# Six strips in work over eight slots, TensorE kept in program order, and masked queries on ScalarE in a line-attention stage

## The chip, the cores and the metric

The kernel runs on one core of a Trainium2 chip. The metric is the device time of one execution in microseconds; three executions of the kernel before had a median of 8827.78 us (8826.51 to 8828.34). All data are float32.

The core has a matrix engine (TensorE, PE), a vector engine (VectorE, DVE), an activation engine (ScalarE, ACT), a general engine (GpSimd, POOL) and a queue that issues loads (SyncE, SP). Each works through its own list of instructions in order; semaphores hold an instruction until what it needs is there. TensorE writes to PSUM[...]; the other engines read from there and copy to SBUF.

## The reference

Two layers act on an image `x` of shape (4, 64, 256, 256). The first is a convolution block: layer norm, attention over channels, a gated local branch, then a feed-forward part that ends with a transform of 8 x 8 patches: forward DFT, a weight per frequency, inverse DFT. The second layer is a pair of linear attentions along image lines, first along rows, then along columns, and a two-layer MLP. What matters here is the end of the first layer and the row attention:

```python
        y = gelu(x_gate) * concatenate([x1_2, x2], 1)
        y = _conv1x1(y, out_w)
        ...
        f = jnp.fft.rfft2(p) * fW
        p = jnp.fft.irfft2(f, s=(P, P))
...
    q = elu(x @ wq.T + bq) + 1        # 4 heads, 1 value per head
    k = elu(x @ wk.T + bk) + 1
    v = x @ wv.T + bv                 # 4 heads, 16 values per head
    q = q / q.mean(over the line);  k = k / k.sum(over the line)
    ktv = einsum('brhcd,brhce->brhde', k, v)
    o = einsum('brhcd,brhde->brhce', q, ktv)
    h = xe + o @ wo.T + bo            # xe: the layer's input, x: xe normalized
```

## The kernel before

The program is one fully unrolled list, in five stages that follow one another: `stage_a` and what ends it (attention of the first layer, up to about 1720 us), `stage_c1` (to about 3400 us), `stage_c2` (to about 5040 us), `stage_c3`, the middle stage that is changed (5050 to 6672 us), and `stage_d` (column attention and MLP, to the end). `stage_c3` does the 1x1 convolution `out_w`, the patch transform with the residual, and the row attention. It reads `yd` and `xmd` from DRAM and writes `hd`.

Its unit of work is a strip: 8 image rows of a pair of images. There are 2 pairs and 32 strips in each, so 64 strips, `seq`. A strip passes five generators, one turn of the loop after another:

- `product`: the convolution, 4 row pairs with two matmuls each (L970, one for each image, each 64 columns of the array wide), a ScalarE copy each (zc, L971); then 16 transposes in four groups (L980) with a copy each (zs, L981).
- `patches`: for both halves of the strip, the forward DFT (L997, two PSUM tiles), times the frequency weights on VectorE (fs, L1001, two), the inverse DFT (L1007, two tiles), the addition of the residual (xe, L1010, two), and the statistics of a layer norm on VectorE and ScalarE (s L1013, xc L1015, square L1017, sv L1018); at the end the root on ScalarE and the reciprocal (rs, L1021 and L1023).
- `features`: four rounds of four transposes (L1033), a copy (xrT, L1035) and four matmuls of scores (L1038), all into one tile qk; then on VectorE the transpose qp (L1043), scale (u, L1045), bias (L1047), the feature map (fe L695, exponential on ScalarE L696, f L1050), kr (L1056), and the masked forms: kx by eight ScalarE instructions (L1058), qx by one GpSimd instruction (L1059); the sums fr (L1061) and, on VectorE, kj and qj twice (L1065, L1066).
- `attend`: 32 small matmuls of keys with values (L1079), the two sums over the line (L1081, L1082), rz and qr (L1084, L1086), zn (L1089), eight transposes of qx (L1095) with copies qT (L1096), a fold (L1100), zT (L1102), and, in the helper `mix`, a matmul (L702), m4 (called m in the profile, L708), its sum mx_m (L710), and then bdm (L1106).
- `update`: four tiles that are first filled with the bias by four matmuls (L1115), then eight matmuls (L1119); VectorE adds xe (h, L1121) and GpSimd issues four transfers to `hd` (L1125).

Turn n runs `patches` of strip n-1, `update` of n-4, `attend` of n-3, `features` of n-2 and `product` of n, in this order, and `_steps` takes one step of each in rotation, from `yield` to `yield`, until all are done. Loads for strip n+1 are issued by SP at the turn's start (ya L955, xmp L957). A scheduler then places the instructions of all engines: it may move an instruction ahead of others of its engine, and did so with TensorE's: in the program as built the four row-pair products of L970 stand as one matmul, then four of L1038, then three of L970.

PSUM has two pools: six tiles tagged `mm` that all matmul groups take in rotation, in the order in which the code asks for them, and two tagged `sm` for qk and zp. SBUF pool `pf` has two buffers for most names, three for xe, one for zc and h1.

Of the kernel before, what the change touches and what calls it, by code (L numbers as in the profile page):

```python
# [249 lines left out]
def kernel(ctx: ExitStack, tc: tile.TileContext, x, packs, fd, out, off):  # L250
# [670 lines left out]
    def stage_c3():  # L921
        NS = H // 8
        with ExitStack() as cs:
# [33 lines left out]
                SY.dma_start(xmp, xmd[pr, s])  # L957
                ld[pr, s] = ya, xmp

            zss, xes, fes, bds = {}, {}, {}, {}  # L960

            def product(pr, s):

                ya, _ = ld[pr, s]

                zc = p.tile([128, 32, 32, 2], F32, name="zc", bufs=1)
                for r in range(4):
                    t = mm()
                    for b in (0, 1):
                        T.matmul(t[b * 64:(b + 1) * 64, :], owT, ya[:, :, 2 * r:2 * r + 2, b * 64:(b + 1) * 64].rearrange("p f y t -> p y f t"), start=True, stop=True)  # L970
                    S.copy(zc[:, :, 8 * r:8 * r + 8].rearrange("p j f t -> p f j t"), t.rearrange("p (f j t) -> p f j t", f=8, t=2))  # L971
                    if r % 2:
                        yield
                zs = p.tile([128, 16, 2 * C], F32, name="zs")
                zss[pr, s] = zs
                for k in range(4):
                    t = mm()
                    for i in range(4):
                        j = 2 * (4 * k + i)
                        T.transpose(t[:, i * 128:(i + 1) * 128], zc[:, j:j + 2].rearrange("p j f t -> p (j f t)"), ident)  # L980
                    S.copy(zs[:, 4 * k:4 * k + 4].rearrange("p g c -> p (g c)"), t)  # L981
                    if k % 2:
                        yield

            def patches(pr, s):

                _, xmp = ld.pop((pr, s))
                zs = zss.pop((pr, s))
                xe = p.tile([128, 16, 2 * C], F32, name="xe", bufs=3)
                sv = p.tile([128, 32], F32, name="sv")  # L990
                for hf in (0, 1):

                    zh = zs[:, 8 * hf:8 * hf + 8].rearrange("p (n g) c -> p n (g c)", n=2)
                    ts = [mm(), mm()]
                    for pt in (0, 1):
                        for n in (0, 1):
                            T.matmul(ts[pt][n * 64:(n + 1) * 64, :], dfw[pt * 64:(pt + 1) * 64, :], zh[pt * 64:(pt + 1) * 64, n], start=True, stop=True)  # L997
                    fs = []
                    for pt in (0, 1):
                        f_ = p.tile([128, 512], F32, tag=f"fs{pt}", name=f"fs{pt}", bufs=1)  # L1000
                        V.tensor_tensor(f_.rearrange("p (g c) -> p g c", c=C), ts[pt].rearrange("p (g c) -> p g c", c=C), mid_bc(fw, 8), ALU.mult)  # L1001
                        fs.append(f_)
                    yield
                    ts = [mm(), mm()]
                    for pt in (0, 1):
                        for n in (0, 1):
                            T.matmul(ts[n][pt * 64:(pt + 1) * 64, :], dfi[n * 64:(n + 1) * 64, :], fs[pt][n * 64:(n + 1) * 64, :], start=True, stop=True)  # L1007
                    for n in (0, 1):
                        r = slice(8 * hf + 4 * n, 8 * hf + 4 * n + 4)
                        V.tensor_tensor(xe[:, r].rearrange("p g c -> p (g c)"), ts[n], xmp[:, r].rearrange("p g c -> p (g c)"), ALU.add)  # L1010
                    src = xe[:, 8 * hf:8 * hf + 8].rearrange("p g (b c) -> p (g b) c", b=2)
                    s1 = p.tile([128, 16], F32, name="s1")
                    V.tensor_reduce(s1, src, AX.X, ALU.add)  # L1013
                    xc = p.tile([128, 16, C], F32, name="xc")
                    V.scalar_tensor_tensor(xc, bc(s1, C), -LN_S, src, ALU.mult, ALU.add)  # L1015
                    sq = p.tile([128, 16, C], F32, name="sq")
                    S.activation(sq, xc, AF.Square)  # L1017
                    V.tensor_reduce(sv[:, 16 * hf:16 * hf + 16], sq, AX.X, ALU.add)  # L1018
                    yield
                sd = p.tile([128, 32], F32, name="sd")  # L1020
                S.activation(sd, sv, AF.Sqrt, bias=eps_t, scale=LN_S)  # L1021
                rs = p.tile([128, 32], F32, name="rs")
                V.reciprocal(rs, sd)  # L1023
                xes[pr, s] = xe, rs

            def features(pr, s):

                xe, rs = xes[pr, s]
                qk = sm()
                for k in range(4):  # L1030
                    t = mm()
                    for i in range(4):
                        T.transpose(t[:, i * 128:(i + 1) * 128], xe[:, 4 * k + i], ident)  # L1033
                    xT = p.tile([128, 512], F32, name="xrT")
                    S.copy(xT, t)  # L1035

                    for g in range(4):
                        T.matmul(qk[g * 32:(g + 1) * 32, k * 128:(k + 1) * 128], rw, xT.rearrange("p (j n) -> p j n", j=4)[:, :, g * 32:(g + 1) * 32],  # L1038
                                 start=True, stop=True)
                    yield  # L1040

                qp = p.tile([128, 16, 32], F32, name="qp")
                V.transpose(qp.rearrange("p j m -> p (j m)"), qk)  # L1043
# [12 lines left out]
                V.tensor_tensor(kr, f[:, :, 4:8], bc(rs, 4), ALU.mult)  # L1056
                for y in range(8):
                    S.activation(kx[:, :, y], kr, AF.Identity, scale=rmask[:, y:y + 1])  # L1058
                G.tensor_tensor(qx, f[:, :, 0:4].unsqueeze(2).to_broadcast([128, 32, 8, 4]), mk.to_broadcast([128, 32, 8, 4]), ALU.mult)  # L1059
                fr = p.tile([128, 2, 8], F32, name="fr")  # L1060
                V.tensor_reduce(fr, f.rearrange("p (j b) h -> p b h j", b=2), AX.X, ALU.add)  # L1061
                qj = p.tile([128, 2, 2, 8, 4], F32, name="qj")
# [6 lines left out]
            def attend(pr, s):  # L1069

                xe, _ = xes.pop((pr, s))
                qx, kx, qj, kj = fes.pop((pr, s))
                yield
                zp = sm()

                for j in range(16):
                    for b in (0, 1):
                        g = (2 * b + j % 2) * 32
                        T.matmul(zp[g:g + 32, :64], kx[:, 2 * j + b].rearrange("p y h -> p (y h)"), xe[:, j, b * 64:(b + 1) * 64], start=(j < 2), stop=(j >= 14))  # L1079
                qs = mm()  # L1080
                T.matmul(qs[:, 0:1], qj.rearrange("p d b y h -> p (d b y h)"), K0("ones"), start=True, stop=True)  # L1081
                T.matmul(qs[:, 1:2], kj.rearrange("p b d y h -> p (b d y h)"), K0("ones"), start=True, stop=True)  # L1082
                rz = p.tile([128, 1], F32, name="rz")
                V.reciprocal(rz, qs[:, 1:2])  # L1084
                qr = p.tile([128, 1], F32, name="qr_")
                V.tensor_copy(qr, qs[:, 0:1])  # L1086
                zn = p.tile([128, 65], F32, name="zn")
                G.memset(zn[:, 64:65], 0.5)
                V.tensor_scalar(zn[:, 0:64], zp[:, 0:64], rz, None, ALU.mult)  # L1089
                qT = p.tile([128, 1024], F32, name="qTr", bufs=1)  # L1090
                for k in (0, 1):
                    t = mm()
                    for i in range(4):
                        j = 8 * k + 2 * i
                        T.transpose(t[:, i * 128:(i + 1) * 128], qx[:, 2 * j:2 * j + 4].rearrange("p a y h -> p (a y h)"), ident)  # L1095
                    S.copy(qT[:, k * 512:(k + 1) * 512], t)  # L1096
                yield
                t = mm()

                T.matmul(t[:65, :64], zn, K("rfold"), start=True, stop=True)  # L1100
                zT = p.tile([65, 2, 64], F32, name="zT")
                V.tensor_copy(zT, mid_bc(t[:65, :64], 2))  # L1102
                yield
                m = mix(p, zT.rearrange("p j y -> p (j y)"), rgt, qr)
                bdm = p.tile([128, 4, 64], F32, name="bdm")
                V.tensor_tensor(bdm, mid_bc(m, 4), bc(K("jmask"), 64), ALU.mult)  # L1106
                bds[pr, s] = xe, qT, bdm

            def update(pr, s):

                xe, qT, bdm = bds.pop((pr, s))
                h1 = p.tile([128, 2, 16, C], F32, name="h1", bufs=1)
                ts = [mm() for k in range(4)]
# [9 lines left out]
                for b in (0, 1):  # L1123
                    for a in (0, 1):
                        G.dma_start(hd[2 * pr + b, 8 * s:8 * s + 8, 8 * a:8 * a + 8], h1[a * 64:(a + 1) * 64, b])  # L1125
                yield

            seq = [(pr, s) for pr in range(B // 2) for s in range(NS)]
            load(*seq[0])

            for n in range(len(seq) + 4):
                if n + 1 < len(seq):
                    load(*seq[n + 1])
                _steps(*(f(*seq[n - d]) for d, f in ((1, patches), (4, update), (3, attend), (2, features), (0, product)) if 0 <= n - d < len(seq)))

    stage_c3()

# [272 lines left out]
```

## Time and profile before

| What | Value |
|---|---|
| median of three executions | 8827.78 us |
| profiled execution, its own time | 8823.91 us |
| its span | 8822.1 us |
| mean granted TensorE clock | 0.971 |
| TensorE busy | 8201.0 us, 93% |
| VectorE busy | 5913.9 us, 67% |
| ScalarE busy | 4597.9 us, 52% |
| GpSimd busy | 1205.3 us, 14% |
| first L970 to last L1121 (the middle stage) | 5051.6 to 6671.6 us |
| L1079 in it, 4096 matmul records | 219 ns each |
| L1059 in it, 64 instructions on POOL | 1967 ns each |

The span is the time from the first to the last instruction of the profiled execution; what lies around it (1.8 us here) belongs to the execution's own time. A float32 matmul makes two matmul records in the profile, a transpose one. Records overlap:[...] the step from one start to the next is the better measure of what it costs TensorE. PE is the matmul engine and PEld its weight loads. A row of the timeline has start, length, engine, line, operation, output and inputs, and in brackets the idle time before it and what ended it. A row of the waits has who waited, for whom, the total in us, how often and the longest.

### The profile page before, as it was taken

Reading aid. Unit: us, or ns where it says so; the run is one execution under the profiler, and the core shown is the slowest. Engines: PE = TensorE matmul, PEld = TensorE weight load, DVE = VectorE, ACT = ScalarE, POOL = GpSimd, SP = SyncE. Lnnn points to the kernel's source line nnn. Section 1 sums busy time; section 2 is a strip of 40 time slices with the busy share of each in tenths; the row PEclk is TensorE's granted clock in tenths of the full one; section 3 lists DMA queues with packets and bytes.
Section 4 is the critical chain, followed back from the end, with each engine's and each line's share of the span. In section 5 each row is a group of like instructions: output and inputs, shape, how many; then the busy total and the mean of one; then the engine's idle time right before and its main releaser. Section 6 shows DMA issues by size and latency. Waiting matters only on the chain. (4 is left out here: it accounts for less than half of the span.)

```text
span 8822.1 us, 143300 instructions
## 1 busy us (share of the span) xinstructions
PE 8201.0 (93%) x57518; PEld 4222.1 (48%) x57518; DVE 5913.9 (67%) x8506; ACT 4597.9 (52%) x7781; POOL 1205.3 (14%) x1828
## 2 busy tenths in 40 slices
PE   8999999699999998999999999999997999999998
PEld 6777777344444443333333344444444444444443
DVE  7766666377777774222222288888887788887886
ACT  4455455455555553222222266666664777777776
POOL 1111111212222221000000011111110101001011
PEclk9999999699999999999999999999997999999999
DMA  7777777799999998888888855555542323333232
GB/s 163 160 188 189 178 185 179 195 351 391 397 386 392 388 388 315 299 295 299 295 299 295 279 174 167 169 168 172 170 142 71 68 58 76 59 66 69 58 76 40
DMA packets 1258502, 1832.48 MB, mean 208 GB/s; under 512 B 335600, under 2 KB 1040112, under 8 KB 1196656
## 3 DMA queue, kind: packets, MB, share of 16 engines
q1 hardware_dynamic: 1053296, 1034.63, 39.0%
q0 software_dynamic: 204544, 788.69, 28.0%
q8 instruction: 456, 7.47, 0.3%
q14 instruction: 206, 1.69, 0.1%
HBM read 967.65 MB, written 788.53 MB: 199 GB/s over the span
## 5 line engine op out<-in xcount | busy, mean ns | idle before, releaser
L915 DVE TENSOR_TENSOR y<-ge,mm 128x512 f32<-128x512 f32 (+1 forms) x640 | 406.0, 635 | 1211.9 <-ACT ge L914 1211.8
L882 PE MATMUL mm<-t,w 128*128 128x512 f32 (+1 forms) x2560 | 1093.9, 566 | 19.4 <-DMA t<-td 19.4
L914 ACT ACTIVATE ge<-mm 128x512 f32<-128x512 f32 (+1 forms) x640 | 354.9, 555 | 1253.5 <-PE mm L889 1253.5
L775 PE MATMUL mm<-gp,wc 128*64 128x510 f32 (+1 forms) x3072 | 702.5, 595 | 91.0 <-DVE xm L785 51.7
L620 PEld LDWEIGHTS mm<-wqk,gp 128*128 128x128 f32 x6144 | 728.8, 197 | 99.4 <-issue 61.5
L882 PEld LDWEIGHTS mm<-t,w 128*128 128x128 f32 x2560 | 455.4, 190 | 647.9 <-issue 437.2
L620 PE MATMUL mm<-wqk,gp 128*128 128x128 f32 x6144 | 762.5, 282 | 1.1 <-POOL gp L589 0.9
L1341 ACT ACTIVATE hg<-mm,b 128x512 f32<-128x512 f32 x1024 | 645.2, 689 | 47.3 <-PE mm L1339 45.6
L1339 PE MATMUL mm<-xfT,w 64*128 64x512 f32 x2048 | 623.7, 626 | 25.7 <-DVE h L1309 22.6
L830 ACT COPY tb<-mm 128x512 f32<-128x512 f32 x512 | 300.7, 588 | 628.0 <-PE mm L824 620.3
L889 PE MATMUL mm<-t,w 64*64 64x504 f32 (+1 forms) x5120 | 575.6, 555 | 0.0
L824 PE MATMUL mm<-xl,pack_c 64*128 64x512 f32 x2048 | 510.6, 599 | 6.4 <-ACT xl L812 4.7
L775 PEld LDWEIGHTS mm<-gp,wc 128*64 128x64 f32 x3072 | 277.2, 137 | 471.1 <-issue 333.6
L1356 PE MATMUL mm<-hg,pack_d 128*64 128x512 f32 x2048 | 496.8, 606 | 0.0
L316 ACT ACTIVATE ln_sq<-xn 128x1024 f32<-128x1024 f32 x256 | 274.6, 1073 | 365.3 <-DVE xn L314 365.2
L1363 POOL DMA_DIRECT2D out_dram<-st x128 | 209.1, 1638 | 1725.0 <-DVE st L1357 1640.9
L318 DVE TENSOR_REDUCE ln_v<-ln_sq 128x16 f32<-128x1024 f32 x256 | 312.0, 1219 | 185.2 <-ACT ln_sq L316 185.2
L970 PE MATMUL mm<-ya,pack_e 128*64 128x512 f32 x1024 | 381.2, 616 | 11.0 <-DMA ya<-yd 11.0
L828 DVE COPY tb<-mm 128x512 f32<-128x512 f32 x512 | 344.2, 683 | 22.4 <-PE mm L824 16.9
L1339 PEld LDWEIGHTS mm<-xfT,w 64*128 64x128 f32 x2048 | 225.6, 185 | 255.2 <-issue 112.1
L1357 DVE TENSOR_SCALAR st<-mm,pack_d 128x512 f32<-128x512 f32 x256 | 277.7, 1085 | 101.3 <-PE mm L1356 101.3
L889 PEld LDWEIGHTS mm<-t,w 64*64 64x64 f32 x5120 | 158.1, 132 | 374.4 <-issue 374.4
(458 smaller groups left out, 15368.5 us busy)
## 6 DMA issues: line engine op xcount, KB each, us to landing
t<-td SPq DMA_DIRECT2D x256, 1152.0 KB, 10.1
td<-tb POOLq DMA_DIRECT2D x144, 1024.0 KB, 15.6
td<-tb POOLq DMA_DIRECT2D x288, 512.0 KB, 13.9
yd<-y POOLq DMA_DIRECT2D x128, 1152.0 KB, 10.1
ya<-yd SPq DMA_DIRECT2D x192, 512.0 KB, 5.7
xs<-in_x_dram SPq DMA_DIRECT2D x128, 512.0 KB, 6.8
projd<-pj POOLq DMA_DIRECT2D x256, 256.0 KB, 5.9
gp<-projd SPq DMA_DIRECT2D x128, 512.0 KB, 9.1
```

Of the source, the lines that this page charges most:

```text
L620: T.matmul(qp[:, k * 128:(k + 1) * 128], gp[:, 2 * i + k // 2, at + dx:at + dx + 128], wqk[:, dx, :], start=(dx == 0), stop=(dx == 2))
L775: T.matmul(tv[i * 64:(i + 1) * 64, :, o], wc[2 * pr + i][:, dx, :], gps[i][:, 2 * r:2 * r + 2, i_], start=(dx == 1), stop=False, skip_grou ...
L824: T.matmul(t, inT[q, hf * 128:(hf + 1) * 128], xls[b // 2, s][q, :, 2 * y:2 * y + 2].rearrange("p f y t -> p f (y t)"), start=True, stop=True)
L828: V.tensor_copy(o, i_)
L882: T.matmul(t[:, :n], w[:, 0:128], x_[:, c, :], start=True, stop=False, skip_group_check=True)
L889: T.matmul(t[po:po + 64, :n].rearrange("p (n c) -> p n c", c=64)[:, :, o], w[q:q + 64, 128:192], x_[q:q + 64, c, i_], start=False, stop=Tr ...
L914: S.activation(ge[:, :n], ts[0][k][:, :n], AF.Gelu)
L915: V.tensor_tensor(y[:, c, :].rearrange("p n c -> p (n c)"), ge[:, :n], ts[1][k][:, :n], ALU.mult)
L970: T.matmul(t[b * 64:(b + 1) * 64, :], owT, ya[:, :, 2 * r:2 * r + 2, b * 64:(b + 1) * 64].rearrange("p f y t -> p y f t"), start=True, sto ...
L1339: T.matmul(t, w1[rh * 64:(rh + 1) * 64, k * 128:(k + 1) * 128], xT[rh * 64:(rh + 1) * 64], start=True, stop=True)
L1341: S.activation(g, t, AF.Gelu, bias=b1[:, k:k + 1])
L1356: T.matmul(y[rh * 64:(rh + 1) * 64, :], w2[:, k, :], hg[k * 2 + rh], start=False, stop=(k == 1), skip_group_check=True)
```

## The change

The change rewrites the yields of `stage_c3`, so that a turn has eight slots, and splits `attend`: its end (the call of `mix` and bdm) becomes a sixth generator, `mixed`, which runs at the start of the next turn. `update` starts in the second slot, `features` makes its next transposes in the slot of the scores before, `attend` starts in the fifth slot. All of the loop stands in a block that takes TensorE's instructions out of the scheduler's hands: they stay as the program has them. The order of the generators in a turn changes. xe gets a fourth buffer. qx is made by eight ScalarE instructions, as kx is, in place of one on GpSimd. The matmuls and their sizes are the same.

```diff
-            zss, xes, fes, bds = {}, {}, {}, {}
+            zss, xes, fes, zts, bds = {}, {}, {}, {}, {}
...
                     S.copy(zc[...], ...)
-                    if r % 2:
+                    yield
+                    if r == 0:
                         yield
+                yield
...
-                xe = p.tile([128, 16, 2 * C], F32, name="xe", bufs=3)
+                xe = p.tile([128, 16, 2 * C], F32, name="xe", bufs=4)
...
                         fs.append(f_)
+                    yield
                     yield
...
                     V.tensor_reduce(sv[:, 16 * hf:16 * hf + 16], sq, AX.X, ALU.add)
                     yield
+                    if hf == 0:
+                        yield
...
-                for k in range(4):
+
+                def up(k):
                     t = mm()
                     for i in range(4):
                         T.transpose(t[:, i * 128:(i + 1) * 128], xe[:, 4 * k + i], ident)
                     xT = p.tile([128, 512], F32, name="xrT")
                     S.copy(xT, t)
+                    return xT
+
+                def score(k, xT):
                     for g in range(4):
                         T.matmul(qk[...], rw, xT..., start=True, stop=True)
-                    yield
+
+                xT = up(0)
+                for k in range(3):
+                    yield
+                    yield
+                    score(k, xT)
+                    xT = up(k + 1)
+                yield
+                score(3, xT)
...
-                G.tensor_tensor(qx, f[:, :, 0:4].unsqueeze(2).to_broadcast([128, 32, 8, 4]), mk.to_broadcast([128, 32, 8, 4]), ALU.mult)
+                for y in range(8):
+                    S.activation(qx[:, :, y], f[:, :, 0:4], AF.Identity, scale=rmask[:, y:y + 1])
...
-                yield
+                for k in range(4):
+                    yield
                 zp = sm()
...
+                yield
                 qs = mm()
...
                     S.copy(qT[:, k * 512:(k + 1) * 512], t)
                 yield
+                yield
                 t = mm()
...
                 V.tensor_copy(zT, mid_bc(t[:65, :64], 2))
-                yield
+                zts[pr, s] = xe, qT, zT, qr
+
+            def mixed(pr, s):
+                xe, qT, zT, qr = zts.pop((pr, s))
                 m = mix(p, zT.rearrange("p j y -> p (j y)"), rgt, qr)
...
                 bds[pr, s] = xe, qT, bdm
+                yield
...
+                yield
                 xe, qT, bdm = bds.pop((pr, s))
...
-                yield
...
-            for n in range(len(seq) + 4):
-                if n + 1 < len(seq):
-                    load(*seq[n + 1])
-                _steps(*(f(*seq[n - d]) for d, f in ((1, patches), (4, update), (3, attend), (2, features), (0, product)) if 0 <= n - d < len(seq)))
+            with tc.manual_schedule(engines={mybir.EngineType.PE}):
+                for n in range(len(seq) + 4):
+                    if n + 1 < len(seq):
+                        load(*seq[n + 1])
+                    _steps(*(f(*seq[n - d]) for d, f in ((4, mixed), (1, patches), (4, update), (2, features), (3, attend), (0, product)) if 0 <= n - d < len(seq)))
```

## The prediction, made before the changed kernel ran

> **What bounds the kernel now.** I read the page's totals and slices, then the middle stage by windows, then one turn of it in order of time, then the waits. The stage runs from the first L970 at 5051.6 us to the last L1121, at 6671.6: 1620 us for 64 turns. In full turns L702 follows L702 after 24.84 us. One turn by windows (length, then busy time of PE, weight loads, DVE, ACT, POOL, then granted clock, DMA share, GB/s):
>
> ```profile
> 5816.00:5840.84 24.84, 23.49 (x218) 12.29 (x217) 21.25 (x41) 15.45 (x29) 4.28 (x6) 1.00 0.55 170
> ```
>
> TensorE is occupied in 23.49 of 24.84 us at full clock; VectorE is next; DMA is half used. The timeline of that turn (start, length, engine):
>
> ```profile
> 5816.95 1.07 PE L970 MATMUL mm<-ya,pack_e 128*64 128x512 f32 x2
> ...
> 5818.39 0.43 PE L1038 MATMUL sm<-xrT,rw 128*32 128x128 f32 x8 [0.36 <-ACT xrT L1035]
> ...
> 5818.74 1.93 PE L970 MATMUL mm<-ya,pack_e 128*64 128x512 f32 x6
> ...
> 5820.07 1.97 POOL L1059 TENSOR_TENSOR qx<-f,pack_e 128x1024 f32<-128x1024 f32 x1
> 5820.39 1.74 DVE L1065 TENSOR_TENSOR kj<-fr,pack_e 128x64 f32<-128x64 f32 x1
> ...
> 5822.05 0.21 DVE L1066 TENSOR_TENSOR qj<-fr,pack_e 128x64 f32<-128x64 f32 x1
> ...
> 5822.39 1.10 PE L1079 MATMUL sm<-xe,kx 128*32 128x64 f32 x64 [0.69 <-ACT kx L1058]
> ```
>
> L1038 splits the two pairs of L970 products, and kj takes 1.74 us while POOL makes qx, 0.21 afterwards. The waits of 5200 to 6560 (55 turns) name what TensorE stands for:
>
> ```profile
> PEld sm L1038 <- ACT xrT L1035: 146.2, 219, 1.2
> ...
> PE sm L1079 <- ACT kx L1058: 38.2, 55, 0.7
> ...
> PE sm L1038 <- ACT xrT L1035: 19.4, 54, 0.4
> ```
>
> A last view, from the first stage, shows what a pause of TensorE does: 1.9 us without a matmul (425.8 to 427.7), then 3.4 us at half clock.
>
> ```profile
> 425.80:428.00 2.20, 0.30 (x9) 0.28 (x10) 2.17 (x4) 0.00 (x0) 0.00 (x0) 0.99 0.23 69
> 428.00:431.40 3.40, 3.40 (x35) 1.62 (x32) 1.46 (x3) 0.76 (x3) 0.00 (x0) 0.50 0.00 0
> 431.40:434.80 3.40, 3.40 (x35) 3.28 (x36) 1.62 (x2) 1.71 (x6) 0.00 (x0) 1.00 0.41 108
> ```
>
> [...]
>
> **The change, part by part.** Durations are steps from start to start in the timelines of before; lines are those of before, and the order is that of the changed program as built.
>
> *TensorE's order.* L970's four products now stand as one, two together, one, whole. Split halves cost 1.00+1.86 us twice a turn, 5.7 in all; unsplit, two products take 1.87 us (in the stage's fill, 5061.22 to 5063.09), one 1.02 (as L997): 3.9. That removes 1.8. The waits on kx (0.7), on xrT (0.4 once, 0.15 twice) and on bdm (0.15) should go too: 1.4 to 1.5. The new order's floor: L702 0.6, L997 two groups 2.0, L1007 two 2.0, L1033 four 2.3, L1038 four 1.4, L970 3.9, L1115 1.0, L1119 3.6, L1079 1.0, L1081 and L1082 0.5, L1095 1.0, L980 1.9, L1100 0.2: 21.4, with changes of shape about 21.6 us.
>
> *qx.* POOL loses 1.97 us, VectorE the 1.53 by which kj is held: 19.7 us left. (Bounds: POOL keeps its hd issues and a 0.1 us memset, so part of the 1.53 could stay, and then lies in the ring below; the second kj, beside those issues, takes 0.21, so I take all of it as gone.) ScalarE gains 8 instructions of L1058's form and size; their step is 0.29, or at most L1058's whole 0.39 if reading f, whose rows are spaced, is slower. I take 0.29: 2.3, so 17.8. They stand behind kx and ahead of the copies xrT(0) and zc(0). kr ends about 3.8 us after L702 starts; 16 x 0.29 makes 8.5, xrT 9.1, zc 9.6. The first L1007 wants xrT's buffer at 10.6 below: hidden with 1.5 us spare (0.7 at 0.39); in a 21.6 us turn it would be late. The last three hd transfers on POOL no longer stand behind qx (2.0 us earlier), and nothing waits for them. SP's loads keep their order.
>
> *xe's fourth buffer* adds no instruction; zero. Without it the first xe write would wait for the last h addition, which VectorE's order puts before it anyway.
>
> *mix in the next turn.* L702 now opens the turn, behind zT, which ends the previous turn on VectorE. Behind L702 on TensorE queue L997, L1033, L970, L1115.
>
> *The new wait.* PSUM has six mm buffers. From L702 on, they are taken by L997 (two), L1033, L970, then four by L1115; so the fourth L1115 takes the buffer that fs1 reads. VectorE's order puts that fs1 last: zT, u+bias, fe, sv, m4, fs0, f, mx_m, kr, fr, bdm, rs, kj, qj, kj, qj, fs1. L1119 stands behind that L1115, so it now waits not for bdm but for fs1; behind it waits the whole rest of the turn, and VectorE for it. This closes a ring:
>
> - VectorE, from the second half's xe to zT: xe 0.60+0.71, s 1.14, qp 0.63, xc 1.13, u 0.33, zT 0.28 = 4.8. (L1100's product is there 2 us earlier.)
> - VectorE, zT's end to fs1's: u+bias starts 0.08 before it, 0.44, fe 0.28 (it waits shortly for ScalarE's square), sv 1.12, m4 0.33, fs0 0.60, f 0.33, mx_m 0.51, kr 0.21, fr 0.50, bdm 0.33, rs 0.26, three of kj and qj 0.39, the last 0.13, fs1 0.68 = 6.0.
> - TensorE, from there to the second L1007's output: L1115 0.95, L1119 3.6, L1007 1.03, L1038 0.38, L1033 0.58, L970 1.88, L997 1.03, L1038 0.38, L1033 0.58, L1079 1.03, L970 1.01, L1081 and L1082 0.49, L1095 0.95, L1007 1.15 = 15.0.
>
> With two handovers of 0.05: 25.9 us. Inside it TensorE stands from 4.1 (three L1115 streamed) to 6.05 us after L702, 1.95 us, and from its last L980 to the next L702, 1.6 us. Ring against before: +1.1 a turn.
>
> *The clock.* The trace of before has no such pause in a full turn, so I bound this: none halved, 0; every first pause halved, 3.4 us at half rate, +1.7 a turn. [...]the second pause now and then slows the opening matmuls, which removes the first. I take 0.8 a turn, so 26.75.
>
> *Sum.* Fill and drain lose waits: the last three intervals, traced 26.3, 22.0 and 12.5, have no closed ring; I estimate -15 in all from the shorter order there (-20 to -5). 60 full turns x (26.75-24.84) = +115; +100 in sum. The other stages' orders are unchanged, so the profiled execution's 8823.91 (span 8822.1 and 1.8 around it) becomes about 8924. The median of the runs, 8827.78, lies 3.9 above that: 8928.
>
> **The rivals.**
> - *The order works* (faster). TensorE runs at its floor, with 0.3 for leftovers 21.9: 60 x (-2.94) - 15 = -191, 8637. For it: VectorE has only 19.7 us of work. Against: VectorE's order is fixed. It decides where fs1 is ready when TensorE has streamed three L1115, 4.1 us after L702 instead of 6.0, and zT 1.6 us earlier too: 3.6 us off the ring's VectorE legs.
> - *Ring without halving* (slower): 60 x 1.1 - 15 = +51, 8879. For: the pauses are just near the size that was punished.
> - *Ring, halved nearly every turn* (slower): 60 x 2.8 - 15 = +153, 8981; for: the pause repeats each turn.
> - *The ring but shorter by 0.9* (small overlaps I count too long): 60 x 0.2 - 15, about no change.
>
> **Numbers.** Ring with part of the turns halved 60%, without halving 15%, halved nearly always 12%, order works 10%, about no change 3%. The range takes in the two slower neighbours, 8868 to 8990, and leaves out 13%. What this kernel's measurement can tell from no change is 0.2%, 18 us. Slower 0.87, same 0.03, faster 0.10.
>
> **What would show it.** Right: L702 every 26 to 27.5 us; the first L1119 of a turn starting about 1 us after fs1's end and never earlier; TensorE pausing twice a turn; granted clock of the stage near 0.97 (half for 3.4 us in about half of the turns); kj at 0.21; VectorE busy about 19.7 a turn. Wrong: L702 at 22 us and L1119 right behind bdm; or VectorE taking fs1 ahead of kj. If L702 is at 25.9 throughout and the clock 1.00, only the clock's share fails.

## The result and the profile after

The changed kernel takes 9033.22 us (median of 4 runs, 9028.23 to 9041.06) against 8828.06 us (4 runs) before: a ratio of 1.0234, 95% interval 1.0219 to 1.0248. It is slower by 205 us. The forecast was slower, by 100 us, with a range that ended at 8990.

The profiled execution took 9030.88 us with a span of 9029.1. These are its totals and its clock, where before had 8201.0 us for PE and nines in the slices that now show eights:

```profile
PE 8350.0 (92%) x57518; PEld 4307.3 (48%) x57518; DVE 5864.9 (65%) x8506; ACT 4743.7 (53%) x8293; POOL 1078.5 (12%) x1764
...
PEclk9999999799999999999999988888887999999999
```

The same number of matmul records keeps TensorE busy 149 us longer, and seven slices of the middle stage stand at 8 in the clock. VectorE has 49 us less. The six of the title are generators: `mixed` and `update` take the same strip, n-4, so five strips are in work in a turn, as before. The middle stage lasts from the first L970 at 5050.8 us to the end of the last h at 6880.2, so 1829 us where it was 1620: the 209 us are all in it. Line numbers below are those of the changed kernel: L1142 is the bias matmul (L1115 before), L1146 the product with bdm (L1119), L1010 the inverse DFT (L1007), L1003 fs (L1001), L1123 zT (L1102), L1013 xe (L1010). By windows, full turns and then four successive stretches of one turn that starts at 5246.6:

```profile
5200.00:6700.00 1500.00, 1374.55 (x11394) 721.89 (x11394) 1075.09 (x2046) 929.16 (x1882) 121.80 (x264) 0.88 0.47 148
```

```profile
5246.60:5249.70 3.10, 3.10 (x18) 1.09 (x18) 3.06 (x7) 3.05 (x4) 0.00 (x0) 1.00 0.97 386
5249.70:5253.10 3.40, 1.84 (x10) 0.60 (x8) 2.76 (x10) 3.39 (x12) 0.00 (x0) 1.00 0.00 0
5253.13:5256.50 3.37, 3.37 (x8) 2.10 (x7) 0.44 (x1) 2.94 (x9) 0.00 (x0) 0.50 0.02 5
5256.55:5259.90 3.35, 3.35 (x9) 2.63 (x9) 1.32 (x3) 0.00 (x0) 0.00 (x0) 0.50 0.00 0
```

The granted clock of full turns is 0.88, where it was 1.00: its records show 0.50 or 1.00, so TensorE spends 24% of the time at 0.50, two stretches of 3.4 us in a turn. In the turn shown, they come one after the other, right behind the stretch of the bias matmuls. Over the 60 full turns there are 122 of them, by the clock's records: one behind the bias matmuls in every turn, a second one right after it in 22 turns, and one behind TensorE's pause ahead of L702 in 40. The order of events in the turn shown:

```profile
5246.24 0.28 DVE L1123 COPY zT<-mm 65x128 f32<-65x128 f32 x1
...
5246.57 0.70 PE L702 MATMUL mm<-rgt,zT 65*128 65x256 f32 x2 [1.60 <-DVE zT L1123]
...
5249.82 1.13 PE L1142 MATMUL mm<-pack_e,one 1*128 1x512 f32 x6
5250.70 0.41 DVE L1131 TENSOR_TENSOR bdm<-mx_m,pack_e 128x256 f32<-128x256 f32 x1
5251.30 0.16 DVE L1083 TENSOR_TENSOR kj<-fr,pack_e 128x64 f32<-128x64 f32 x1
...
5251.77 0.69 DVE L1003 TENSOR_TENSOR fs<-mm,fw 128x512 f32<-128x512 f32 x1
...
5252.51 1.51 PE L1142 MATMUL mm<-pack_e,one 1*128 1x512 f32 x2 [1.56 <-DVE fs L1003]
...
5253.95 6.67 PE L1146 MATMUL mm<-bdm,qTr 128*128 128x256 f32 x16
```

This is the ring that was forecast: L702 waits for zT; three bias matmuls stream; the fourth waits for fs1, which VectorE does last; bdm is ready at 5251.1 and L1146 starts only at 5253.95. What was not forecast is that L1146's sixteen records take 6.67 us; before, the same sixteen took 3.72, 1.3 us after the first bias matmul:

```profile
5811.58 1.14 PE L1115 MATMUL mm<-pack_e,one 1*128 1x512 f32 x8
...
5812.87 3.72 PE L1119 MATMUL mm<-bdm,qTr 128*128 128x256 f32 x16
```

The waits of 52 full turns (5200 to 6700) name the same two places, and no third, for TensorE's matmuls:

```profile
PE mm L702 <- DVE zT L1123: 83.2, 52, 1.6
...
PE mm L1142 <- DVE fs L1003: 41.7, 46, 1.6
```

The mean step from L702 to L702 over the 60 full turns is 28.54 us, the shortest 27.58 and the longest 30.33; before it was 24.84.

### The profile page after: what moved, and what is told of

The parts are those of the page before. It is cut to its first block, busy times and chain, and to the rows that moved or that the text cites. A ratio compares the mean times of both kernels' runs of the same rounds, so it can differ in the third digit from the quotient of the medians.

```text
span 9029.1 us, 143626 instructions
## 1 busy us (share of the span) xinstructions
PE 8350.0 (92%) x57518; PEld 4307.3 (48%) x57518; DVE 5864.9 (65%) x8506; ACT 4743.7 (53%) x8293; POOL 1078.5 (12%) x1764
## 3 DMA queue, kind: packets, MB, share of 16 engines
q0 software_dynamic: 204544, 788.69, 27.1%
## 4 chain that ended last, share of the span: by engine, by line
PE 56%; DVE 29%; ACT 9%; issue 3%; DMA 2%; POOL 0%; SPq 0%; DVEq 0%; ACTq 0%; POOLq 0%
PE mm L882 12%; PE mm L889 6%; PE mm L1146 4%; PE mm L775 4%; PE mm L620 4%; DVE ln_s L1208 3%; DVE v L1216 3%; DVE xc L1210 3%; PE mm L824 3%; ACT xl L812 2%; ACT ln_sq L316 2%; PE mm L970 2%; DVE st L1384 2%; DVE xn L314 2%; PE mm L1366 2%
## 5 line engine op out<-in xcount | busy, mean ns | idle before, releaser
L1148 DVE TENSOR_TENSOR h<-mm,xe 128x512 f32<-128x512 f32 x256 | 177.1, 692 | 315.5 <-PE mm L1146 313.1
L1041 ACT COPY xrT<-mm 128x512 f32<-128x512 f32 x256 | 148.6, 581 | 429.8 <-PE mm L1039 429.8
L1146 PE MATMUL mm<-bdm,qTr 128*128 128x256 f32 x1024 | 371.5, 541 | 0.5 <-DVE bdm L1131 0.5
L828 DVE COPY tb<-mm 128x512 f32<-128x512 f32 x512 | 344.9, 685 | 22.3 <-PE mm L824 16.8
```

Source lines behind the costliest of these rows:

```text
L1146: T.matmul(t[:, i * 256:(i + 1) * 256], qT[:, (2 * k + i) * 128:(2 * k + i + 1) * 128], bdm.rearrange("p j e -> p (j e)"), start=False, st ...
```

## Experiments

All times are medians with the ratio to the kernel before, run on the same chip beside each experiment (8823.75 to 8825.88 us there; the first row is the one beside the changed kernel); "turn" is the mean step from L702 to L702 over 60 full turns, and "clock" the granted clock from 5200 to 6400 us.

| Kernel | us | ratio (95% interval) | turn, us | clock |
|---|---|---|---|---|
| before | 8828.06 | 1 | 24.84 | 1.00 |
| changed | 9033.22 | 1.0234 (1.0219 to 1.0248) | 28.54 | 0.88 |
| bias with 32 rows | 8937.3 | 1.0126 (1.0111 to 1.0141) | 27.06 | 0.93 |
| fold one slot earlier | 8751.9 | 0.9916 (0.9899 to 0.9932) | 23.73 | 0.93 |
| fourth bias late | 8857.67 | 1.0038 (1.0023 to 1.0053) | 25.58 | 0.96 |
| qx on GpSimd | 9166.1 | 1.0387 (1.0372 to 1.0403) | 30.72 | 0.86 |
| fold earlier, bias with 32 rows | 8651.89 | 0.9802 (0.9788 to 0.9815) | 22.22 | 1.00 |
| scheduler keeps TensorE | 9030.49 | 1.0232 (1.0218 to 1.0246) | 28.55 | 0.88 |
| before, qx on ScalarE | 8853.24 | 1.003 (1.0019 to 1.0041) | 25.38 | 1.00 |
| fold earlier, bias with 8 rows | 8653.93 | one run | 22.21 | 1.00 |
| fold earlier, bias with 2 rows | 8706.92 | one run | 23.14 | 0.96 |
| fold earlier, 32 rows, 31 of them zero | 8662.11 | one run | 22.22 | 1.00 |
| fold earlier, 32 rows, qx on GpSimd | 8676.4 | 0.9831 (0.9814 to 0.9847) | 22.67 | 1.00 |

The theory after the result was: the ring is as forecast, 25.9 us, and the rest of the turn is the clock, halved more often than the pauses would explain, with the bias matmuls, which read one row each, as the cause. The rival: pauses alone, counted wrongly.

### Bias with 32 rows

```diff
-            V.memset(one, 1.0)
+            V.memset(one, 1.0 / 32)
...
-                    T.matmul(ts[k], one[k * 32:k * 32 + 1, :], K("rowbo8")[k * 32:k * 32 + 1, :], ...)
+                    T.matmul(ts[k], one[k * 32:k * 32 + 32, :], K("rowbo8")[k * 32:k * 32 + 32, :], ...)
```

> The changed kernel, with each bias matmul reading 32 rows of ones/32 and of the (repeated) bias in place of one row: same four matmuls, same place, same length, same sum. Theory A (a matmul of one row does not count as work for what grants the clock, so each turn has 3.8 us of apparent idleness from the first bias matmul to L1146, 3.2 to 7.0 us after L702): half-clock stretches fall from about two a turn to below one, the granted clock of the stage rises from 0.88 to about 0.96, a turn falls from 28.5 to 26.5-27.1 us, in all 8915-8950 us. Rival B (the pauses of 1.7-1.9 us alone halve the clock, and I only counted their chance too low): no change, 28.5 us a turn and 9030 us. In both, a turn that meets no halving would be 25.9.

Measured: 8937.3 us, 27.06 us a turn (the upper edge of what was expected), clock 0.93 (0.96 was expected). Full turns of the experiment by windows, against 0.88 above:

```profile
5200.00:6400.00 1200.00, 1086.44 (x9541) 564.74 (x9540) 902.86 (x1721) 781.36 (x1587) 102.98 (x224) 0.93 0.49 155
```

Nothing but the number of rows read was changed (and the ones, to 1/32), and 96 us went. The rival falls as the whole cause. The half-clock stretches of the 60 turns fell from 122 to 64 (1.07 a turn; below one was expected). Behind the bias matmuls they fell from 82 to 33, and 21 turns have one there in place of all 60; ahead of L702 they fell from 40 to 31. All that remain begin behind a window with a pause of 1.45 to 1.6 us, or behind another half-clock stretch.

The turns that no halving slows take 25.94 us (25.9 forecast). One whole stretch on the ring's TensorE leg makes it 27.6 (+1.65), two make it 29.3. The turns from 26.1 to 27.1 have none on that leg: there the stretch behind the pause ahead of L702 slows the opening matmuls and fs1 ends up to 1.1 us later. In the mean, a turn of this experiment is 25.9 plus 0.9 for stretches on the leg and 0.2 for late openings; a turn of the changed kernel is 25.9 plus 2.3 and 0.3.

The changed kernel's own trace agrees. In the clock's records all its changes stand, to within 0.02 us, on one grid with a step of 3.413 us; a window, here and below, is one step of that grid. In the 60 turns, 380 windows ran at full clock. The 100 that were followed by half clock held at most 1.82 us of matmuls other than the bias ones, the other 280 at least 1.81. With the bias matmuls counted in, the two groups overlap: some of the 100 were filled to 3.36 us.

### Fold one slot earlier

```diff
                     S.copy(qT[:, k * 512:(k + 1) * 512], t)
-                yield
                 yield
                 t = mm()
```

> The changed kernel without one of attend's two yields ahead of the fold (L1121), so that the fold and zT come one slot earlier, ahead of the strip's last transposes. Theory (the ring through VectorE's zT and fs1 sets the turn): zT is ready before the norm's xc on VectorE, L702 no longer waits, fs1 is done about when TensorE has streamed the first bias matmuls; TensorE near its floor of 21.6, a turn 22.3-23.2 us, few half-clock stretches, in all 8660-8720 us. Rival (VectorE's own work, or ScalarE's, sets the turn): zT moves but L702 to L702 stays above 26 us, 8900 us or more.

Measured: 8751.9 us. The ring is open: the first turns take 22.21 us and TensorE never pauses, as expected. The time was missed all the same, because from the seventh full turn on every turn takes 23.9 us. A turn of that kind in this experiment (L1141 is its bias matmul, L1145 its product with bdm), and its stretches by windows:

```profile
5390.12 1.08 PE L970 MATMUL mm<-ya,pack_e 128*64 128x512 f32 x4
5391.13 1.94 PE L1141 MATMUL mm<-pack_e,one 1*128 1x512 f32 x8
5393.00 5.41 PE L1145 MATMUL mm<-bdm,qTr 128*128 128x256 f32 x16
```

```profile
5388.00:5411.90 23.90, 23.90 (x219) 13.11 (x218) 20.14 (x40) 17.91 (x37) 2.29 (x5) 0.93 0.55 170
5390.10:5393.50 3.40, 3.40 (x15) 1.27 (x15) 3.40 (x7) 2.94 (x5) 0.00 (x0) 1.00 0.83 318
5393.51:5396.90 3.39, 3.39 (x9) 2.70 (x9) 1.98 (x6) 2.87 (x7) 0.00 (x0) 0.50 0.03 7
```

TensorE is busy in all of the 3.40 us ahead of the halving, 1.9 of them with bias matmuls, and is halved. No pause is left that could be blamed. The two kinds of turn differ in where in a window the bias matmuls stand: in the 54 halved turns the first of them starts 1.02 to 1.40 us into a window, in the six turns before, which were not halved, at 0.87 to 0.97 or at 2.59 to 2.71. A turn of 22.2 is 6.5 windows, so the place jumps from turn to turn; 22.2 with half a stretch added is 23.9, and that is seven times 3.413, so a halved turn brings the next one to nearly the same place: the turn has locked to seven windows. That these numbers meet I take for chance.

### Fourth bias late

```diff
-                for k in range(4):
+                for k in range(3):
                     T.matmul(ts[k], one[...], K("rowbo8")[...], start=True, stop=False, ...)
                 for k in range(4):
                     t = ts[k]
+                    if k == 3:
+                        T.matmul(t, one[96:97, :], K("rowbo8")[96:97, :], start=True, stop=False, ...)
```

> The changed kernel with the fourth bias matmul moved behind the third tile's products, so that the first three tiles' products do not stand behind the buffer that fs1 reads. Theory (the wait on fs1 is part of the ring): L1146 of the first tile starts right after bdm, 4.7 us after L702 in place of 7.0; the lone bias matmul costs 1.0, so a turn without halving is 24.7, with the halvings that stay 25.3-26.2, in all 8815-8875 us. Rival (fs1's wait hides under bdm's): nothing gained and 1.0 lost, 29.5 us a turn, 9090 us.

Measured: 8857.67 us, 24.79 us for a turn without halving, 25.58 in the mean, all three as expected. In its timeline the product with bdm (L1148 here) starts when bdm ends, and not when fs1 does; the lone bias matmul is L1146:

```profile
5163.44 0.41 DVE L1131 TENSOR_TENSOR bdm<-mx_m,pack_e 128x256 f32<-128x256 f32 x1
...
5163.91 2.86 PE L1148 MATMUL mm<-bdm,qTr 128*128 128x256 f32 x12 [0.22 <-DVE bdm L1131]
5166.69 1.12 PE L1146 MATMUL mm<-pack_e,one 1*128 1x512 f32 x2
```

So the wait of the fourth bias on fs1's buffer is part of the ring: without halving the turn falls from 25.94 to 24.79, although the lone matmul costs 1.05 (5166.69 to the next start at 5167.74). The rest of the 3.0 us a turn that went is the clock's, 0.96 where it was 0.88: no stretch follows the bias matmuls any more.

### qx on GpSimd

```diff
-                for y in range(8):
-                    S.activation(qx[:, :, y], f[:, :, 0:4], AF.Identity, scale=rmask[:, y:y + 1])
+                G.tensor_tensor(qx, f[...].to_broadcast([128, 32, 8, 4]), mk.to_broadcast([128, 32, 8, 4]), ALU.mult)
```

> The changed kernel with qx made by one GpSimd instruction again. Theory (kj lies in the ring, so the 1.5 us by which GpSimd's qx holds it come back into the turn): kj about 1.7 us long, a turn 29.5-30.9 us, in all 9090-9170 us. Rival (ScalarE's eight instructions are a cost, in the way of xrT and zc): faster than the changed kernel, a turn below 28, below 9000 us.

Measured: 9166.1 us, 30.72 us a turn, kj up to 1.36 us long (about 1.7 was expected). The move of qx to ScalarE helps the changed kernel by 133 us; it is not what made it slow. (The granted clock is 0.86 here and 0.88 in the changed kernel, so the 2.2 us a turn are not kj's alone.)

### Fold earlier and bias with 32 rows

The two edits above together.

> The fold one slot earlier and the bias matmuls with 32 rows, together. Theory (ring broken, and what is left of the half-clock stretches comes from the one-row matmuls alone, since TensorE has no pause): every turn 22.1-22.3 us, granted clock 1.00 in the stage, in all 8645-8675 us. Rival (the lock of the turn to 23.9 us has another cause[...]): 23.9 us and 8750 us as before.

Measured: 8651.89 us, every turn 22.2 to 22.3 us. Full turns by windows, then a window whose bias matmuls start 1.13 us into it, and the next:

```profile
5200.00:6400.00 1200.00, 1199.98 (x11668) 644.36 (x11664) 1074.33 (x2107) 947.55 (x1945) 123.74 (x270) 1.00 0.61 191
...
5199.63:5203.03 3.40, 3.40 (x16) 1.22 (x15) 3.40 (x7) 2.96 (x5) 0.00 (x0) 1.00 0.91 358
5203.05:5206.44 3.39, 3.39 (x20) 2.72 (x22) 1.98 (x6) 2.87 (x7) 0.00 (x0) 1.00 0.01 2
```

```profile
5199.76 1.08 PE L970 MATMUL mm<-ya,pack_e 128*64 128x512 f32 x4
5200.76 1.95 PE L1141 MATMUL mm<-pack_e,one 32*128 32x512 f32 x8
```

The window looks like the one ahead of the halving above, with bias matmuls as long (1.95 us for 1.94), and the next one runs at full clock. Nor is it luck of the place: this run's bias matmuls start at places all over the window, never more than 0.14 us apart, nine of them between 1.02 and 1.41.

TensorE is busy throughout at full clock, VectorE in 19.9 of 22.2 us. It beats both kernels: 2.0% under before (interval 1.85 to 2.12%), 4.2% under the changed one (8651.89 / 9033.22). A full TensorE as the cause of the lock falls: it is busy for 1199.98 of 1200 us here as in the run with the fold earlier, with 11668 matmul records in them where that run had 10838, and no turn is halved.

### Scheduler keeps TensorE

```diff
-            with tc.manual_schedule(engines={mybir.EngineType.PE}):
-                for n in range(len(seq) + 4):
+            for n in range(len(seq) + 4):
```

> The changed kernel without the block that takes TensorE from the scheduler; yields, sixth generator, qx and buffers as changed. In the built program TensorE's order in a turn then differs from the changed kernel's only in one matmul of L970 ahead of L1098. Theory (the yields and the split, not the hold on the order, make the ring): a turn as in the changed kernel, 28-29 us, 9000-9050 us. Rival (the fixed order alone costs the time): near the kernel before, 8830-8900 us.

Measured: 9030.49 us and 28.55 us a turn, the changed kernel's own numbers. With these yields, the hold on TensorE's order neither costs nor gains.

### Before, qx on ScalarE

```diff
-                G.tensor_tensor(qx, f[...].to_broadcast([128, 32, 8, 4]), mk.to_broadcast([128, 32, 8, 4]), ALU.mult)
+                for y in range(8):
+                    S.activation(qx[:, :, y], f[:, :, 0:4], AF.Identity, scale=rmask[:, y:y + 1])
```

> The kernel before with qx made by eight ScalarE instructions; nothing else. Theory (in before's order L1095 follows 1.5 us after L1079, which waits for kx, so eight more instructions at 0.29 us behind kx are seen by TensorE as a wait, while the 1.5 us that VectorE's kj wins is off the path): slower by 0.3-0.7 us a turn, 8840-8870 us. Rival (VectorE's order passes the 1.5 us on to TensorE): faster by up to 1 us a turn, 8765-8825 us.

Measured: 8853.24 us, 25.38 us a turn: slower by 0.54 a turn, as expected, but the path is not quite the one I gave. In its timeline (L1060 is qx, L1080 the small matmuls that were L1079):

```profile
5814.40 0.69 ACT L1060 ACTIVATE qx<-f,pack_e 128x128 f32<-128x128 f32 x2 [1.23 <-DVE f L1050]
5815.00 2.43 ACT L1058 ACTIVATE kx<-kr,pack_e 128x128 f32<-128x128 f32 x8
...
5817.48 1.10 PE L1080 MATMUL sm<-xe,kx 128*32 128x64 f32 x64 [0.96 <-ACT kx L1058]
...
5818.76 0.36 PE L1083 MATMUL mm<-pack_k,kj 128*128 128x1 f32 x2
...
5819.23 0.86 PEld L1096 LDWEIGHTS mm<-pack_k,qx 128*128 128x128 f32 x8 [0.20 <-ACT qx L1060]
5819.24 1.09 PE L1096 MATMUL mm<-pack_k,qx 128*128 128x128 f32 x8
```

Two of qx's eight run ahead of kx, since they need f alone, and kx ends 2.74 us after kr where it was 2.48; TensorE waits 0.96 us there (0.69 before). The other six end at 5819.18, and the transposes of qx (L1096) wait for them: they start 0.48 us after L1083, where it was 0.23 before. Together that is 0.52 of the 0.54.

### How many rows, and whether zeros count

Three variants of the kernel with the fold earlier: 8 rows of ones/8, 2 rows of ones/2, and 32 rows of which the stationary operand has ones in the first and zeros in the others. The edit for 8 rows, and the one for the zeros:

```diff
-            V.memset(one, 1.0)
+            V.memset(one, 1.0 / 8)
...
-                    T.matmul(ts[k], one[k * 32:k * 32 + 1, :], K("rowbo8")[k * 32:k * 32 + 1, :], ...)
+                    T.matmul(ts[k], one[k * 32:k * 32 + 8, :], K("rowbo8")[k * 32:k * 32 + 8, :], ...)
```

```diff
-            V.memset(one, 1.0)
+            V.memset(one, 0.0)
+            for k in range(4):
+                V.memset(one[k * 32:k * 32 + 1, :], 1.0)
```

> The fold one slot earlier, each bias matmul with 8 rows of ones/8. What counts as work for the clock: if rows count in proportion, the bias stretch counts as a quarter, which is just enough or just not enough (0.58 of the stretch before the halving): turns of 22.2 or a mixture; if a matmul on fewer rows than a full group of 32 counts as nothing, turns of 23.9 as with one row; if anything over one row counts in full, 22.2 throughout.

> The fold one slot earlier, each bias matmul with 2 rows of ones/2. If rows count in proportion to a group of 32, 2 rows count as 6% of the bias stretch: turns of 23.9 us as with one row, 8750 us. If what fails to count is the one-row matmul alone, 22.2 and 8655 us as with 8 rows.

> The fold one slot earlier, each bias matmul with 32 rows of which 31 have zero in the stationary operand (the bias rows stay as they are). If rows that are read count, whatever their weights: 22.2 us and 8655 us as with 32 rows of ones/32. If only rows with non-zero weights count: 23.9 us and 8750 us.

With 8 rows: 22.21 us in every turn, as with 32. With 32 rows of which 31 have zero weights: 22.22, as with ones/32 in all of them (the moving rows were not set to zero). Four turns of the first and seven of the second have their bias matmuls at the place where one row was halved, 1.02 to 1.41 us into a window, and were not.

With 2 rows the first 33 turns take 23.9 and the later 27 take 22.2, which neither expectation had. The window with the bias matmuls in a turn of the first kind, and the next window:

```profile
5198.60:5202.00 3.40, 3.40 (x16) 1.19 (x15) 3.40 (x7) 2.97 (x5) 0.00 (x0) 1.00 0.80 322
5202.01:5205.40 3.39, 3.39 (x9) 2.70 (x8) 1.98 (x6) 2.87 (x7) 0.00 (x0) 0.50 0.01 2
```

The place tells the two kinds apart. In the 33 halved turns the bias matmuls start 1.22 to 1.41 us into a window; the next turn starts at 1.42, is not halved, and with 22.2 us a turn the place then moves away and does not come back between 1.02 and 1.41. So two rows were halved wherever they met the place of one row, and the run shows no difference between the two; no one-row turn starts as late as 1.42. One and two rows were halved, 8 and 32 not; whether rows count in proportion was not shown.

### Fold earlier, 32 rows, qx on GpSimd

The kernel of 8651.89 us with the edit of "qx on GpSimd" above.

> The fold one slot earlier and 32-row biases, but qx on GpSimd again: what the move of qx is worth once the ring is open. Theory (VectorE is held by 1.5 us again and has 21.4 of 22.2 us to do, so part of it reaches TensorE): 22.6-23.4 us a turn, 8675-8735 us. Rival (hidden in VectorE's spare 2.3 us): 22.2 us and 8655 us.

Measured: 8676.4 us, 22.67 us a turn. In the open ring the move of qx is worth 24.5 us (8676.4 less 8651.89).

## Why the prediction was wrong

Step by step, in the prediction's order.

- *TensorE's order*: right as a floor. With the ring open a turn takes 22.21 us; 21.6, or 21.9 with leftovers, was forecast.
- *qx*: right. kj fell to 0.21 us, and in the changed kernel nothing on TensorE waits for qx. Its worth is 133 us in the ring and 24.5 outside of it; in before's order the same move costs 29 us (8853.24 less 8824.67). VectorE is busy 20.5 us a turn (1075.09 of 1500 us), where 19.7 was worked out.
- *mix in the next turn* and *the new wait*: right, in place and size. The turn that starts at 5246.6 us has the two VectorE legs at 4.80 us (xe at 5270.99 to zT's end at 5275.79) and 5.94 (zT's end at 5246.52 to fs1's at 5252.46), forecast 4.8 and 6.0. Turns that no halving slows take 25.94 in the run with 32 rows; 25.9 was forecast. The two experiments that open the ring at its two ends (zT, fs1) shorten the turn by what they should.
- *The clock*: this step failed. I wrote: "I bound this: none halved, 0; every first pause halved, 3.4 us at half rate, +1.7 a turn", and took 0.8; how many pauses would be halved was my estimate, with one pause of before's first stage behind it (1.9 us, then 3.4 us at half clock). Measured is 28.54 less 25.9, 2.6 us a turn, above my upper bound. The third leg of the turn shown, from fs1's end to the second half's xe, lasts 18.5 us where 15.1 was forecast, and the two half-clock stretches in it (6.8 us at half rate, 3.4 lost) are the difference. The error of 1.8 a turn over 60 turns is 108 us, and the forecast was 105 short.

What the step had wrong is, first, what it took for a pause. It counted the time between matmuls, 1.95 us. The run with 32 rows shows that the one-row bias matmuls belong with it: read as 32 rows, they had 33 half-clock stretches behind them where there had been 82. Pause and bias matmuls together, from the first of these to L1146, take 3.8 to 4.3 us in the 20 turns whose opening ran at full clock, 2.2 to 4.2 in the 40 whose slowed opening brought the bias matmuls closer to fs1's end. The window ahead of the first stretch held 2.08 us or more of pause and bias matmuls in each of the 60 turns, and all 60 were halved; the step's estimate was about half of them. Of the 2.6 us, about 1.1 (27.06 less 25.9) stay with 32 rows, so the single rows cost 1.5 us a turn.

Second, the bound left out that one stretch can follow another: in 22 of the 60 turns a second one came, in 12 of the 21 halved ones with 32 rows. The lone fourth bias matmul, which stands across the start of the first stretch (1.44 us from its start to L1146's in the turn shown, 1.05 in the run that has it late), is my reading of why; no run tested it. Third, the stretch behind the pause ahead of L702 was counted as a help that spares the first stretch; in the changed kernel it spared none, and cost 0.3 us a turn. For true pauses the step's 0.8 was near the 1.1 measured, but by luck: with 32 rows a third of the turns was halved on that leg and not about half, but more than half of these twice.

The stage's trace of before gave no warning: its four bias matmuls and the wait behind them take 1.3 us from start to start, with other matmuls on both sides, and none of its 60 full turns was halved (clock 1.00).

- *Fill and drain*: forecast -15. The last three steps are 53.1 us against 60.8 before, 8 less, and the fill, from the first L970 to the first L702, is 55.4 against 60.9, 5 less: about right.
- *The rivals*: "ring, halved nearly every turn" had the right picture and, by the same bound, too small a number, 8981. "The order works" failed here by one yield: with it gone, 8751.9, and with the clock kept up, 8651.89 (8637 was worked out for that rival).

## What to carry to other kernels

Ahead of a change of order, follow who frees each buffer in rotation: one matmul that only prepares a tile waited here for the last reader of a buffer, and what stood behind it on TensorE waited too (L1146 began 2.8 us after bdm was ready). Where a loop runs through two engines in turn, add its legs: 25.9 us here, where the busiest engine's sum was 21.6. Watch groups of matmuls that read one or two rows: with the fold earlier, TensorE's records busy throughout, half clock followed the four bias matmuls in 54 of 60 turns with one row (1.9 us of them), in 33 of 60 with two, and in none with 8 or 32. In before, where the four one-row matmuls took 1.3 us from start to start between others, it followed in none either. So such a group is worth a try in smaller pieces or with more rows.

## What the runs showed of the hardware that was not expected

A group of four one-row matmuls of 512 columns (1.9 us in a 3.41 us window, TensorE otherwise busy) was followed by 3.41 us at half clock in the 54 turns of the run with the fold earlier in which it started 1.02 to 1.40 us into a window. With 2 rows the same followed in all 33 turns with a start from 1.22 to 1.41; with 8 or 32 rows, zero weights among them, it did not follow at the same places. A loop that was halved once a turn locked to a multiple of the window: 23.9 us, seven times 3.413, in 54 of the 60 turns of the run with the fold earlier.
